# Two more blocks of queries turned by DMA, and gates' weights shared by both halves of a batch

## The chip, the core and the metric

The kernel runs on one core of a Trainium2 chip. The metric is the device time of one execution in microseconds (us). The engines of a core work side by side, each through its own queue in order: TensorE (PE, with its weight loads PEld), VectorE (DVE), ScalarE (ACT), GpSimd (POOL) and SyncE (SP), whose queue here issues nearly all DMAs. They wait for each other through semaphores.

## The reference

A transformer layer over 8 sequences of 1024 rows and 512 features, in float32. First attention with 16 heads of 32 features, causal, on the normalized rows, added to the input; then a gated recurrence on the normalized sum, added again. The recurrence runs over the 8 sequences as its time steps; the 1024 rows are its batch.

```python
def attn(query, in_proj_weight, out_proj_weight):        # query: layernorm(x), 8 x 1024 x 512
    q, k, v = ...                                         # 16 heads of 32
    scores = jnp.einsum('bhqd,bhkd->bhqk', q / math.sqrt(D), k)
    scores = jnp.where(causal[None, None], scores, -jnp.inf)
    attn = jax.nn.softmax(scores, axis=-1)
    return jnp.einsum('bhqk,bhkd->bhqd', attn, v) @ out_proj_weight.T   # heads joined first

def step(c, xt):                                          # xt: one sequence of z', 1024 x 512
    ft = jax.nn.sigmoid(xt @ wf.T + c @ uf.T + bf)
    it = jax.nn.sigmoid(xt @ wi.T + c @ ui.T + bi)
    gt = jnp.tanh(xt @ wc.T + c @ uc.T + bc)
    return ft * c + it * gt, None

x = x + attn(layernorm(x))
z = layernorm(x)                                          # z' below
c_final, _ = lax.scan(step, c0, z)
x = x + jnp.tanh(z @ wo.T + c_final @ uo.T + bo)
```

## The kernel before

**Precision.** Every float32 operand of a product is split into two float16 tiles, high and low part, and a product is three matmuls (high x high, high x low, low x high). `three` issues them for four blocks of 128 features: 12 matmuls of 512 columns, in four planned operations of three.

**Stages.** For each sequence b: normalization and a transpose by DMA into tile zT, one per half of 512 rows (`ln1`); projections to q, k and v in four groups of four heads (`proj`); attention for eight pairs P of heads (64 pairs in all); `out_proj`, whose sum with the input is stored as X1, normalized (z') and turned by DMA into tile z2T; and the gates of the recurrence (`recur`). After the last sequence the output stage runs. Gates of one sequence run beside the attention of the next, so that TensorE always has several kinds of work to choose from.

**Attention in two passes.** The first pass (`a_group`, nine groups per pair, listed in GA) computes scores with queries on the partitions, in the PSUM tile sa (one slot of 1024 columns, two banks), and VectorE reduces them to the maximum of each row. `m_rows` turns the maxima and puts them as two more rows under q. The second pass (`b_group`) computes the scores again with keys on the partitions, in the PSUM tile sb (one slot of 1024 columns), now with the maximum subtracted; ScalarE takes exp (tile e), GpSimd sets the masked half of diagonal blocks to zero, and `split_e` makes the two float16 parts (tile P: ScalarE the high, GpSimd the low). `times_v` multiplies these by v, and `finish` divides by the sum. For the first 16 pairs (MASKED) the mask is added by small matmuls of TensorE instead, in both passes.

**Turned rows.** From pair 20 on (TURNED), queries 896 to 1023 of both heads (query block 7) take another way (`turned_rows`): their scores are computed once, with queries on the partitions, in sb; VectorE masks and reduces, ScalarE takes exp with the row's own maximum as bias, `split_e` splits, and a DMA transposes the 128 x 2048 float16 tile into a second slot of P. Their first-pass groups (0, 7) and (1, 7) fall away, and BANKS lists how the other query blocks are packed into sb.

**Gates.** `recur(t)` goes through its two halves of 512 rows one after the other; in each, through four blocks of features and three gates, 12 units. A unit loads its weights from device memory into tile wf (512 KB, two slots), runs 12 matmuls on z2T and, from t = 1 on, 12 on cs, the split state, and ScalarE and VectorE update the state C.

**Order.** The code records every step as an operation with engine, estimated duration, due time `at`, and the buffers that it reads, writes and holds. `Plan.schedule` then writes out each engine's order: it takes again and again the operation that can start first by its own estimates and, among equals, the one due first. Rings (R) have a fixed number of slots; a buffer takes a slot at its first operation. Due times come from TAU, the length of a pair, and t_a, t_b and t_batch, the times of the first pass, the second pass and a batch. The result is one fixed order per engine, which the chip follows. So moved due times or another number of slots change the order everywhere.

Lines in the profile: L519 is `three`, L566 the products of v, L645 first-pass scores, L647 and L755 mask matmuls, L655 masked maxima and L653 plain ones, L712 scores of turned rows, L717 and L718 their maximum and its scaling, L753 second-pass scores, L758 and L721 exp, L730 and L731 the split, L767 masking on GpSimd, L695 `times_v`, L837 the sum after out_proj, L815 the high part of an attention output, L341 and L343 transposing and plain DMAs.

Of the kernel before, what the change touches and what calls it, by code (L numbers as in the profile page):

```python
# [76 lines left out]
class Plan:  # L77
# [3 lines left out]
    def op(self, eng, dur, fn, r=(), w=(), at=0.0, size=None, hold=(), after=(), alt=None, port=None):  # L81
        o = Op()
        o.alt = alt or {}
        o.port = eng == "POOL" if port is None else port
        o.eng, o.dur, o.fn, o.at, o.size, o.seq = eng, dur, fn, at, size, len(self.ops)
        o.pre, o.succ, o.bufs = {}, [], set(hold)
        for p in after:
            o.pre[p] = 1
        for write, items in ((False, r), (True, w)):
            for x in items:  # L90
                b, key = x if isinstance(x, tuple) else (x, None)
                o.bufs.add(b)
                keep = []
                for k, p, pw in b.acc:
                    hit = key is None or k is None or k == key
                    if hit and (write or pw) and p is not o:
                        o.pre[p] = 1
                    if not (write and hit and (key is None or k == key)) or p is o:
                        keep.append((k, p, pw))
                keep.append((key, o, write))  # L100
                b.acc = keep
        for b in o.bufs:
            b.left += 1
        self.ops.append(o)
        return o

    def schedule(self):
# [19 lines left out]
        while left:  # L127
            best = None
            for e, l in avail.items():
                t = clock[e]  # L130
                pick = None
                for o in l:
# [10 lines left out]
                    ok = True  # L143
                    for b in o.bufs:
                        if b.ring is not None and b.slot is None:
                            q = b.ring
                            if not q.free or (q.fifo and q.queue[0] is not b) or any(x.left for x in q.over):
                                ok = False
                                break
                            f = max([min(q.free)[0]] + [x.end for x in q.over])  # L150
# [47 lines left out]
def layer(ctx, tc, x_in, wqkvT, woT, ffn, woffT, uoffT, vecs, bo, inc, out):  # L198
# [58 lines left out]

    def ring(name, n, shape, dtype, fifo=True, pool_=sb):
        return Ring([pool_.tile(shape, dtype, name=f"{name}{i}") for i in range(n)], fifo)

    def cut(raw, at, n, shape, dtype, fifo=True):
# [12 lines left out]
    raw = {n: sb.tile([128, w * 512], F32, name=n) for n, w in (("zsr", 4), ("natr", 4), ("er", 4), ("Pr", 8), ("stkr", 12), ("wxr", 6))}  # L274
    rz = cut(raw["zsr"], 0, 2, [128, 2, 2, 512], F16, False)
    rn = cut(raw["natr"], 0, 2, [128, 2, T], F16)
    re_ = cut(raw["er"], 0, 2, [128, T], F32)
    rp = cut(raw["Pr"], 0, 4, [128, 2, T], F16, False)
# [8 lines left out]
        "zT": ring("zT", 3, [128, 4, 2, KE, 128], F16),  # L287
# [6 lines left out]
        "e": re_,  # L294
        "P": rp,
        "m": ring("m", 2, [128, 2, 8], F32),
        "m1": ring("m1", 4, [128, 2], F32),
# [12 lines left out]
        "sa": ring("sa", 1, [128, T], F32, True, ps2),  # L310
        "sb": ring("sb", 1, [128, T], F32, True, ps2),
# [11 lines left out]
    R["ty"] = Ring(big("er", 1024) + big("Pr", 1024), over=[re_, rp])  # L323
# [11 lines left out]
    def new(tag):  # L335
        return R[tag].buf()
# [10 lines left out]
    TAU = 33  # L347
    X_SH, X_RAMP, X_G = 40, 12, 6
    T0 = 70
# [152 lines left out]
    def ln1(b, after=()):  # L502

        at0 = -300.0 if b == 0 else t_a(18 * G * b) - 2 * TAU - 60.0 - X_SH * max(0.0, 1 - 4 * b / X_RAMP)
# [75 lines left out]
    def stack_load(P):  # L580
# [9 lines left out]
        if p == 0:  # L590
# [4 lines left out]
    MASKED = 16  # L595
# [13 lines left out]
    AHEAD = 12  # L609
    TURN_KB = 900  # L610
    BANKS = [[(1, 0, 4, 3), (1, 3, 4, 1)], [(1, 1, 4, 3), (1, 3, 5, 1)], [(1, 2, 4, 3), (1, 3, 6, 1)],
             [(1, 4, 4, 3), (1, 6, 6, 1)], [(1, 5, 5, 2), (0, 2, 2, 2)], [(0, 1, 1, 3), (0, 3, 3, 1)], [(0, 0, 0, 4)]]

    def turned(P):
        return P >= TURNED

    def a_group(n):

        P, gi = divmod(n, 9)
        if turned(P) and len(GA[gi]) == 1:  # L620
# [82 lines left out]
    def turned_rows(P, h, at):  # L703
# [3 lines left out]
        pp, e, W, m1 = new("sb"), new("e"), new("P"), new("m1")  # L707

        def fn():
            q, k = t()[:96, 0], t()[:96, 1]  # L710
            for lo in (0, 512):
                pe.matmul(pp()[:, lo : lo + 512], q[:, h, 896:1024], k[:, h, lo : lo + 512], start=True, stop=True)  # L712

        op("PE", 0.435, fn, [(t, j) for j in range(3)], [pp], at)

        def top():
            dve.tensor_tensor_reduce(pp(), pp(), tri, 1.0, NEG, ALU.add, ALU.max, m1()[:, 0:1])  # L717
            dve.tensor_scalar(m1()[:, 1:2], m1()[:, 0:1], TSN, ebias, ALU.mult, ALU.add)  # L718

        op("DVE", 1.55, top, s("TS"), [pp, m1], at)  # L720
        op("ACT", 1.2, lambda: act.activation(e(), pp(), AF.Exp, bias=m1()[:, 1:2], scale=TS), [pp, m1, *s("TS")], [e], at)  # L721
# [4 lines left out]
        items = [(lambda hl, kb=kb: T_()[:, hl, kb * 128 : kb * 128 + 128], kb, 7) for kb in range(8)]  # L726
        return lambda at: times_v(s_, 2 * p + h, 1, items, [T_], at)
# [5 lines left out]
    def b_group(P, banks, at):  # L733
# [5 lines left out]
        for i, group in enumerate(banks):  # L739
            off = i * 512  # L740
            for h, j, kb, q0, nq in group:
                if q0 == kb:
                    diag.append(off)
                parts.append((h, j, kb, q0, off, nq * 128))
# [4 lines left out]
        def fn():  # L749
            q, k = t()[:98, 0], t()[:98, 1]  # L750
            for h, j, kb, qb0, off, w in parts:
# [6 lines left out]
        op("ACT", 1.2, lambda: act.activation(e(), pp(), AF.Exp, bias=ebias, scale=TS), [pp, *s("TS")], [e], at)  # L758
# [14 lines left out]
        for h, j, kb, qb0, off, w in parts:  # L773
            items = [(lambda hl, o=off + x * 128: W()[:, hl, o : o + 128], kb, qb0 + x) for x in range(w // 128)]
            times_v(s_, 2 * p + h, j, items, [(W, 0), (W, 1)], at + 4.0)

    def b_pair(P):
        if not turned(P):
            for i, banks in enumerate(GB_):
                b_group(P, [[(h, j, kb, max(kb, 4 * j), 4 * j + 4 - max(kb, 4 * j)) for h, j, kb in g] for g in banks], t_b(9 * P + i))  # L780
            return
        banks = [[(h, *x) for x in b] for h in range(2) for b in BANKS]
        late = []
        for i in range(9):
            at = t_b(9 * P + i)
            if i % 4 == 0 and i < 8:
                late.append(turned_rows(P, i // 4, at - AHEAD))
            else:
                k = 2 * (i - 1 - i // 5)
                b_group(P, banks[k : k + 2], at)  # L790
                if i in (3, 7):
                    late.pop()(at + 4.0)
# [60 lines left out]

    def recur(t):
        start = t_batch(t + 1) + (140 if t == NB - 2 else 50)
        span = 8 * TAU
        tag = "pj" if t < NB - 1 else "pt"
        for half in range(2):
            begin = ()
            for fq in range(KE):  # L860
                c = C[:, fq, half * 512 : half * 512 + 512]
                key = (state, (fq, half))
                for i, g in enumerate((0, 2, 1)):
                    un = fq * 3 + g
                    w = new("wf")
                    at = start + span * (12 * half + fq * 3 + i) / 24
                    dma(w, lambda un=un: SF()[un], at - 8.0, r=[(SF, (un, 0)), (SF, (un, 1))], w=[w], size=512)
                    if fq == i == 0 and t:
                        cs = csplit(t, half, at - 5.0)
                    zt, p = z2T[t, half], new(tag)  # L870
                    three(p, p, lambda b, k, zt=zt: zt()[:, :, b, k], lambda a, k, w=w: w()[:, 0, a, k], 512, lambda k: [zt, w], at, last=t == 0,
                          after=tanh.get((t - 1, half), ()))
                    if t:
                        three(p, p, lambda b, k, cs=cs: cs()[:, b, k], lambda a, k, w=w: w()[:, 1, a, k], 512,
                              lambda k, cs=cs: [(cs, (k, 0)), (cs, (k, 1)), w], at, first=False)
                    bb = bias if t else bias0
                    o = new("g2") if g == 2 else p
                    tanh[t, half] = (op("ACT", 0.75, lambda o=o, p=p, g=g, bb=bb, fq=fq: act.activation(o(), p(), AF.Tanh, bias=bb[:, g, fq : fq + 1], scale=UG[g]),  # L878
                       [p, *s(("gate", g), ("b0", g, fq))], [o], at),)
                    marks.append(tanh[t, half])  # L880
                    if g == 0:
                        if t:
                            op("DVE", 0.7, lambda p=p, c=c: dve.scalar_tensor_tensor(c, p(), 1.0, c, ALU.add, ALU.mult), [p], [key], at)
                        else:
                            op("DVE", 0.7, lambda p=p, c=c, fq=fq: dve.tensor_scalar(c, p(), 1.0, vec[:, 4, fq : fq + 1], ALU.add, ALU.mult),
                               [p, *s("vec")], [key], at, after=cw_ops)
                    elif g == 2:
                        gg = o
                    else:
                        op("DVE", 0.7, lambda p=p, gg=gg: dve.scalar_tensor_tensor(p(), p(), 1.0, gg(), ALU.add, ALU.mult), [gg], [p], at)  # L890
                        op("DVE", 0.7, lambda p=p, c=c: dve.scalar_tensor_tensor(c, p(), 2.0 ** t, c, ALU.mult, ALU.add), [p], [key], at)
# [139 lines left out]
    for s_ in range(NS):  # L1031
# [3 lines left out]
        if g == G - 1:  # L1035
            out_proj(b)
# [4 lines left out]
    END = t_batch(NB) + 240  # L1041
# [27 lines left out]
    dma(bob, lambda: bo.partition_broadcast(128), END, w=[bob])  # L1069
# [109 lines left out]
```

## Time and profile before

| what | value |
|---|---|
| median of 3 runs | 2691.12 us (2685.93 to 2691.55) |
| the profiled execution | 2684.05 us |
| its span, first to last instruction | 2682.0 us |
| mean granted TensorE clock | 0.991 |
| longest wait of TensorE in all, on VectorE's maxima (sa, L645 after L653) | 18.0 us, 27 times |
| DMA, mean | 179 GB/s |
| transposes of probabilities | 88 |
| loads of gates' weights | 192 of 512 KB |

How to read it: a line of a group gives source line, engine, operation, output <- input with tile names, how often, busy time and mean duration. Busy times of matmuls overlap, since they are pipelined, so the distance between starts says more than a duration. A line in order of time has the start, the time from the first start to the last end of the merged instructions, and their number. A wait is named by what waited and what released it last. One unit of the second pass is a `b_group` or a `turned_rows`; each pair has nine.

### The profile page before, as it was taken

What the parts mean: (1) busy time and instruction counts of PE and PEld (TensorE: products, weight loads), DVE (VectorE), ACT (ScalarE), POOL (GpSimd) and SP (SyncE); (2) the same over time, 40 slices, a digit from 0 to 9 for tenths busy, and PEclk for the clock granted to TensorE, in tenths of its full rate; (3) what the DMA queues carried; (4) which work ended last, traced back from release to release, by engine and by line L of the source; (5) the groups of instructions that cost most, each with busy time, mean ns of one, the idle gap of its engine ahead of it and who ended that gap; (6) DMA issues with size and microseconds to landing.
All of it is one profiled execution on the core that took longest, in us unless ns stands there. A gap on an engine that the chain in (4) does not pass through costs nothing. (4 is left out here: it accounts for less than half of the span.)

```text
span 2682.0 us, 59783 instructions
## 1 busy us (share of the span) xinstructions
PE 2599.8 (97%) x23677; PEld 1484.9 (55%) x23677; DVE 1821.0 (68%) x4373; ACT 1835.0 (68%) x2286; POOL 1563.9 (58%) x1214
## 2 busy tenths in 40 slices
PE   5889999999999999999999999999999999999999
PEld 3555665665555555555555555555555555544444
DVE  4898877787776767676676667676676776432455
ACT  3697879887777777777777677776776777522222
POOL 3475777777766667676767666676666767410000
PEclk9899999999999999999999999999999999999999
DMA  8566576557666876688758876687766765574565
GB/s 241 175 173 190 148 189 186 154 165 195 158 160 170 200 190 167 166 190 205 183 147 189 192 193 160 165 201 199 177 153 160 199 162 126 146 200 151 195 228 212
DMA packets 535304, 479.97 MB, mean 179 GB/s; under 512 B 402160, under 2 KB 402160, under 8 KB 531440
## 3 DMA queue, kind: packets, MB, share of 16 engines
q1 hardware_dynamic: 533936, 474.06, 67.5%
q8 instruction: 185, 3.03, 0.5%
q10 hardware_dynamic: 1088, 2.10, 0.2%
q14 instruction: 95, 0.78, 0.1%
HBM read 270.54 MB, written 108.53 MB: 141 GB/s over the span
## 5 line engine op out<-in xcount | busy, mean ns | idle before, releaser
L731 POOL TENSOR_TENSOR Pr<-er,Pr 128x1024 f16<-128x1024 f32 x565 | 1207.6, 2140 | 481.7 <-ACT Pr L730 404.6
L758 ACT ACTIVATE er<-sb,ebias,usc 128x1024 f32<-128x1024 f32 x488 | 586.6, 1202 | 155.5 <-PE sb L753 123.7
L730 ACT ACTIVATE Pr<-er 128x1024 f16<-128x1024 f32 x576 | 605.2, 1054 | 50.0 <-POOL er L767 36.1
L519 PEld LDWEIGHTS <-wf 128*128 128x128 f16 x4320 | 398.6, 97 | 416.9 <-DMA wf<-SF 6.1
L655 DVE CUSTOM_DVE_ANT_0 sa<-sa,tri 128x768 f32<-128x768 f32 (+7 forms) x680 | 478.5, 704 | 174.2 <-PE sa L645 162.1
L519 PE MATMUL pj<-z2T,wf 128*128 128x512 f16 x2016 | 496.5, 379 | 3.7 <-DVE natr L551 1.1
L519 PE MATMUL pj<-cs,wf 128*128 128x512 f16 x1728 | 421.7, 379 | 0.0
L519 PE MATMUL pj<-zT,wxr 128*128 128x512 f16 x1536 | 383.3, 384 | 5.0 <-DMA zT<-zsr 3.3
L695 PEld LDWEIGHTS <-Pr 128*128 128x128 f16 x9216 | 323.6, 96 | 100.3 <-POOL Pr L731 6.2
L695 PE MATMUL av<-vt,Pr 128*128 128x65 f16 (+1 forms) x9216 | 339.9, 185 | 4.3 <-POOL Pr L731 2.8
L645 PE MATMUL sa<-stkr 96*128 96x512 f16 (+3 forms) x1348 | 299.9, 322 | 19.9 <-DVE m L653 18.0
L753 PE MATMUL sb<-stkr 98*128 98x128 f16 (+3 forms) x1624 | 306.8, 296 | 9.3 <-ACT er L758 8.4
L519 PEld LDWEIGHTS <-wxr 128*128 128x128 f16 x1728 | 160.7, 98 | 180.4 <-issue 14.1
L653 DVE TENSOR_REDUCE m<-sa 128x1 f32<-128x256 f32 (+2 forms) x248 | 177.7, 753 | 54.0 <-PE sa L647 53.0
L767 POOL TENSOR_SCALAR_AFFINE_SELECT er<-er 128x256 f32<-128x256 f32 (+2 forms) x384 | 140.1, 383 | 119.0 <-ACT er L758 117.9
L645 PEld LDWEIGHTS <-stkr 96*128 96x128 f16 x1360 | 123.7, 98 | 128.8 <-issue 23.7
L753 PEld LDWEIGHTS <-stkr 98*128 98x128 f16 x1624 | 141.7, 97 | 96.0 <-issue 9.6
L566 PE MATMUL pj<-wxr,zT 128*128 128x128 f16 x3072 | 191.0, 220 | 2.9 <-ACT wxr L425 1.9
L566 PEld LDWEIGHTS <-zT 128*128 128x128 f16 x3072 | 179.0, 99 | 12.8 <-issue 3.7
L453 POOL TENSOR_TENSOR zsr<-z,zsr 128x512 f16<-128x512 f32 x120 | 141.7, 1181 | 70.8 <-ACT zsr L452 64.1
L519 PE MATMUL pj<-wo,aT 128*128 128x512 f16 x768 | 174.2, 379 | 1.1 <-DVE wxr L837 0.8
L717 DVE CUSTOM_DVE_ANT_0 sb<-sb,tri 128x1024 f32<-128x1024 f32 x88 | 108.6, 1234 | 90.7 <-PE sb L712 87.5
(171 smaller groups left out, 2797.3 us busy)
## 6 DMA issues: line engine op xcount, KB each, us to landing
wf<-SF SPq DMA_DIRECT2D x192, 512.0 KB, 4.0
stkr<-QK SPq DMA_DIRECT2D x192, 256.0 KB, 4.8
QK<-natr SPq DMA_DIRECT2D x64, 512.0 KB, 4.7
wxr<-x SPq DMA_DIRECT2D x112, 256.0 KB, 4.2
wxr<-SQ SPq DMA_DIRECT2D x93, 256.0 KB, 3.1
VD<-vs SPq DMA_DIRECT2D x64, 264.0 KB, 2.9
vt<-VD SPq DMA_DIRECT2D x32, 528.0 KB, 5.2
stkr<-X SPq DMA_DIRECT2D x16, 1024.0 KB, 7.3
```

The costliest lines, as they stand in the source:

```text
L453: o = op("DVE", 0.85, lambda: eng[o.eng].tensor_tensor(zs()[:, i, 1], z(), zs()[:, i, 0], ALU.subtract), [z, (zs, (i, 0))], [(zs, (i, 1))] ...
L519: pe.matmul(pv(), sv(a, k), mv_(b, k), start=first and k == 0 and i == 0, stop=last and k == KE - 1 and i == 2)
L566: pe.matmul(p()[:, n * 128 : n * 128 + 128], zt()[:, n, a, k], w[2]()[:, c, k], start=i == 0, stop=i == 3 * KE - 1)
L645: pe.matmul(pp()[:, lo:hi], q[:, h, qb * 128 : qb * 128 + 128], k[:, h, lo - off : hi - off], start=True, stop=not last, skip_group_check= ...
L653: dve.tensor_reduce(m()[:, h, qb : qb + 1], pp()[:, off : off + w], AX.X, ALU.max)
L655: dve.tensor_tensor_reduce(pp()[:, off : off + w], pp()[:, off : off + w], tri[:, T - w :], 1.0, NEG, ALU.add, ALU.max, m()[:, h, qb : qb ...
L695: pe.matmul(av()[:, o + 32 * hl : o + 65], stat(hl), v()[:, kb, i, 32 * hl : 65], start=c == 1, stop=c == total, skip_group_check=True)
L730: op("ACT", 1.06, lambda: act.activation(W()[:, 0], e(), AF.Copy), [e], [(W, 0)], at)
L731: lo = op("POOL", 2.18, lambda: eng[lo.eng].tensor_tensor(W()[:, 1], e(), W()[:, 0], ALU.subtract), [e, (W, 0)], [(W, 1)], at, alt={"DVE": ...
L753: pe.matmul(pp()[:, off : off + w], k[:, h, kb * 128 : kb * 128 + 128], q[:, h, qb0 * 128 : qb0 * 128 + w], start=True, stop=not last, ski ...
L758: op("ACT", 1.2, lambda: act.activation(e(), pp(), AF.Exp, bias=ebias, scale=TS), [pp, *s("TS")], [e], at)
L767: pool.affine_select(out=x, in_=x, pattern=[[0, n], [1, 128]], compare_op=ALU.is_ge, fill=0.0, base=0, channel_multiplier=-1)
```

## The change

- `turned` now lists pairs (head, query block). From pair 20 on, head 0 also has query blocks 6 and 0 (queries 768 to 895 and 0 to 127) turned, from pair 60 on head 1 too. Blocks 6 and 0 are one call of `turned_rows`: 896 and 128 columns side by side in one tile, in sa instead of sb. Their first-pass groups (0, 6)+(0, 0), and (1, 6)+(1, 0), fall away. BANKS has a second packing for a head with three blocks turned, five banks instead of seven. Transposes come 20 units of due time ahead instead of 12, the products 4 behind the due time of the row.
- Tile P has six slots instead of four; zT has two instead of three. e and P lie in one raw buffer.
- In `recur`, except for the last sequence, the units of the two halves alternate, and a unit of half 1 uses the weights that half 0 loaded.
- The mask matmuls end at pair 14 instead of 16.
- Due times: TAU 32.75 instead of 33, T0 76 instead of 70, other ramps at the front, gates due 60 (200 for the last but one) after their batch instead of 50 (140), the end 260 instead of 240 behind. The calls of the second pass and of out_proj are sorted by due time before they are recorded. The planner counts slots when one operation takes several, and keeps buffers in the order of use.

```diff
-    rp = cut(raw["Pr"], 0, 4, [128, 2, T], F16, False)
+    rp = cut(big_, 0, 8 if MERGE else 6, [128, 2, T], F16, False)
+    re_ = cut(big_, 6144, 2, [128, 2, T], F16)
...
-        "zT": ring("zT", 3, [128, 4, 2, KE, 128], F16),
+        "zT": ring("zT", 2, [128, 4, 2, KE, 128], F16),
...
-    TAU = 33
-    X_SH, X_RAMP, X_G = 40, 12, 6
-    T0 = 70
+    TAU = 32.75
+    X_SH, X_RAMP, X_G = 40, 8, 7
+    T0 = 76
...
-    MASKED = 16
+    MASKED = 14
...
-    AHEAD = 12
+    TURNED2 = 20
+    TURNED3 = 60
+    PROMPT = 4
+    AHEAD = 20
...
+        2: [[(0, 1, 4)], [(1, 1, 4)], [(2, 2, 4)], [(3, 3, 3), (5, 5, 1)], [(4, 4, 2), (0, 5, 1), (1, 5, 1)]],
...
     def turned(P):
-        return P >= TURNED
+        if P < TURNED:
+            return []
+        return [(h, q) for h in range(2) for q in ((7, 6, 0) if (P >= TURNED2 and (h == 0 or P >= TURNED3)) else (7,))]
...
-        if turned(P) and len(GA[gi]) == 1:
+        if any(x in turned(P) for x in GA[gi]):
...
-    def turned_rows(P, h, at):
+    def turned_rows(P, h, qbs, at):
...
-        pp, e, W, m1 = new("sb"), new("e"), new("P"), new("m1")
+        pp, e, W, m1 = new(TURN_PS if len(qbs) > 1 else "sb"), new("e"), new("P"), new("m1")
+        parts, off = [], 0
+        for qb in qbs:
+            parts.append((qb, off, qb * 128 + 128))
+            off += qb * 128 + 128
...
+        def exps():
+            for i, (qb, off, w) in enumerate(parts):
+                act.activation(e()[:, off : off + w], pp()[:, off : off + w], AF.Exp, bias=m1()[:, 2 + i : 3 + i], scale=TS)
...
+            for x, qbs in enumerate(((7,), (6, 0))[: two[h]]):
+                if PROMPT < 0:
+                    turn(h, qbs, a0 + x * step - AHEAD, end - 0.5 * step + 4.0 + 0.1 * x)
+                else:
+                    turn(h, qbs, a0 + x * step - AHEAD, a0 + x * step + PROMPT)
...
+    SHARE = 1
+
     def recur(t):
-        start = t_batch(t + 1) + (140 if t == NB - 2 else 50)
+        start = t_batch(t + 1) + (200 if t == NB - 2 else 60)
...
+        if t < NB - 1 and SHARE:
+            units = [(half, fq, i, (2 * (3 * fq + i) + half) / 24) for fq in range(KE) for i in range(3) for half in range(2)]
+        else:
+            units = [(half, fq, i, (12 * half + 3 * fq + i) / 24) for half in range(2) for fq in range(KE) for i in range(3)]
+        wfs, css, ggs = {}, {}, {}
+        for half, fq, i, x in units:
...
+            if un in wfs:
+                w = wfs.pop(un)
+            else:
+                w = new("wf")
+                if t < NB - 1 and SHARE:
+                    wfs[un] = w
+                dma(w, lambda un=un: SF()[un], at - 8.0, r=[(SF, (un, 0)), (SF, (un, 1))], w=[w], size=512)
...
-            out_proj(b)
+            events.append((t_batch(b + 1) + 6.0, len(events), out_proj, (b,)))
+    for _, _, fn, a in sorted(events, key=lambda x: x[:2]):
+        fn(*a)
...
-    END = t_batch(NB) + 240
+    END = t_batch(NB) + 260
```

## The prediction

> **What bounds the kernel.** I read the totals first, then the same engines by stretches of the span, then what TensorE waits for, then its instructions in order of time.
>
> ```profile
> PE 2599.8 (97%) x23677; PEld 1484.9 (55%) x23677; DVE 1821.0 (68%) x4373; ACT 1835.0 (68%) x2286; POOL 1563.9 (58%) x1214
> ```
>
> By stretches (columns: stretch, its length, then busy us of TensorE, weight loads, VectorE, ScalarE, GpSimd, the granted clock, the DMA share, GB/s):
>
> ```profile
> 603.00:2144.00 1541.00, 1536.53 (x14441) 885.94 (x14440) 1083.22 (x2832) 1140.92 (x1407) 1037.44 (x863) 1.00 0.73 179
> 0.00:67.00 67.00, 39.79 (x313) 24.12 (x314) 33.15 (x69) 25.38 (x36) 20.67 (x25) 0.97 0.82 241
> 67.00:402.00 335.00, 302.40 (x3433) 195.68 (x3432) 281.34 (x610) 265.97 (x336) 219.63 (x128) 0.93 0.63 175
> 402.00:603.00 201.00, 195.66 (x2157) 121.15 (x2155) 152.74 (x336) 179.70 (x219) 147.83 (x85) 1.00 0.62 169
> ```
>
> From 603 to 2144 us TensorE is idle for 4.5 of 1541 us; ScalarE, the next, is at 74%. The idle time is at the front: 27.2 us before 67, 32.6 us up to 402, where the clock is 0.93 too. A busy row could hide slow, overlapping matmuls, so the distance from start to start is what counts:
>
> ```profile
> 1003.01 2.85 PE L566 MATMUL pj<-wxr,zT 128*128 128x128 f16 x48
> 1005.70 0.60 PE L645 MATMUL sa<-stkr 96*128 96x512 f16 x3
> 1006.13 0.60 PE L753 MATMUL sb<-stkr 98*128 98x384 f16 x4
> 1006.57 2.76 PE L519 MATMUL pj<-z2T,wf 128*128 128x512 f16 x12
> 1009.16 0.60 PE L645 MATMUL sa<-stkr 96*128 96x512 f16 x3
> ```
>
> No gap stands between different tasks. 1024 columns of scores take 0.43 to 0.44 us whether they are three matmuls (1005.70 to 1006.13) or four (1006.13 to 1006.57); twelve of 512 columns take 2.59 us, 216 ns each; 48 of 128 columns take 2.69 us, 56 ns each. So TensorE streams without a pause, and in this stretch the time is the sum of its matmuls. What shortens that sum shortens the span, unless it opens a gap.
>
> **Part 1, queries 6 and 0 turned too.** Head 0 of pairs 20 to 63 and head 1 of pairs 60 to 63: 44 + 4 = 48 times, the first-pass group (6, 0) in tile sa (1024 columns) falls away. Its 1024 columns are now computed once, in turned_rows, and the second pass loses the same two sets of blocks: in the orders of instructions, sa's score matmuls stay as many, sb's lose 48 x 1024 columns. Saved: 48 x 0.435 = 20.9 us of TensorE. The new BANKS also cut 240 matmuls out of sb (longer ones take their place); three or four for 1024 columns cost the same above, so nothing for that.
>
> [...]
>
> What stands against it, off TensorE: the reductions by VectorE move with the rows, plus 48 of L718 (0.273 us) = 13 us; ScalarE's one exp of 1.2 us becomes two (896 wide, about 1.05 by width, and 128 wide, 0.27 as L815's 128-wide copy), 48 x 0.12 = 6 us; GpSimd loses 96 diagonal blocks and wins 32 (Part 3). Of 1541 us these engines use 1083, 1141 and 1037, so all of it is covered: nothing. If that cover were gone, ScalarE's 6 us would count in full.
>
> New waits. A turned row holds sa (its only slot) through 1.10 + 0.30 + 2 x 0.14 + 0.27 us on VectorE and 1.3 on ScalarE, about 3.3 us; queued behind it on TensorE is the next first-pass group, and behind that everything, since the queue is in order. By the changed order, costed with the rows above, the work between is 3.1 us at the least, 3.7 at the lowest tenth, 4.75 in the median. So a few rows stall for tenths: 0 to 48 x 0.5 = 24 us at worst, and I take 1, near 0, because turned rows in sb held it 2.85 us with 2.97 us between at the least, and no sb wait is listed between 603 and 2144 us.
>
> The transposes: 48 more on SP, each 2.9 us of the queue (median of the 88), against 84 loads of wf fewer (0.34 us each). Landing takes these times (median) from the issue:
>
> ```profile
> wf<-SF SPq DMA_DIRECT2D x192, 512.0 KB, 4.0
> Pr<-Pr SPq DMA_TRANSPOSE x88, 5.0
> zT<-zsr SPq DMA_TRANSPOSE x36, 4.9
> z2T<-zsr SPq DMA_TRANSPOSE x28, 5.4
> ```
>
> The longest of the 88 took 9.6 us. By the orders, the TensorE work from issue to first use was at least 7.4 us and is now at least 14.0 (AHEAD 12 to 20), and six P slots instead of four hold the rows meanwhile. Cost: nothing; if landings passed 14 us, TensorE would wait for the excess. The queue's bytes go down (25 MB more in transposes, 44 MB less in wf).
>
> **Part 2, gates' weights shared by both halves.** Matmuls and weight loads on TensorE stay (4320 with wf); only DMA is saved, which nobody waited for (1.0 us in all before 2345). But half 0 and half 1 of the state now advance together, so both z2T slots stay held until a batch's gates end, and out_proj of half 1 comes late. Before, the order left 116 to 132 us of TensorE work between the last product of half 1 and the first gate that reads it (batches 1 to 6); now 16.2 (batches 2 to 5), in batch 0 only 9.6, batch 1 15.5. What this has to cover is seen at one boundary:
>
> ```profile
> 1528.64 2.75 PE L519 MATMUL pj<-wo,aT 128*128 128x512 f16 x12
> 1531.43 0.75 DVE L837 SCALAR_TENSOR_TENSOR wxr<-pj,usc,wxr 128x512 f32<-128x512 f32 x1 [1.12 <-PE pj L519]
> 1537.87 2.33 SPq L341 DMA_TRANSPOSE z2T<-zsr  x1
> ```
>
> The products end at 1531.2, the transpose is issued at 1537.9 and lands 5.4 later: 12.1 us. So 16.2 suffices, and batch 0 stalls 12.1 - 9.6 = 2.5. Half 0 keeps 16 or more there. The last batch: its half 0 leaned on 15.6 us and now has 10.4, because the gates of batch 6 are done before; the same chain there took from 2345.6 (fourth of eight products that begin at 2335.22, 2.59 each) to 2352.5 + 4.9, so 11.8, and stalls 1.4. Together 4 us; the bounds are 0 and the case of rival A.
>
> **Part 3, pairs 14 and 15 masked off TensorE.** 64 mask matmuls fall away at 0.056: 3.6 us; VectorE and GpSimd take the masks (32 blocks of 0.29 us), at 76% and 74% between 402 and 603. Nothing for that; if ScalarE, at 89% there, sets that stretch instead, the 3.6 us are lost.
>
> **Part 4, due times and rings** (TAU, T0, ramps, recur's starts, two zT slots). They only reorder. By the orders, 15.7 us of filler on TensorE (eight products of proj, eight of v, eight of out_proj) move from before to behind the 81st unit of the second pass, that is, out of the stretch that has gaps. If VectorE and ScalarE set the pace there, TensorE idles up to 15.7 us longer; if not, nothing, and better packing could win some of the 32.6 idle. TensorE at 90%, ahead of VectorE at 84%, is the nearest row: I take 0, with -10 to +15.7 for the range. zT's two slots leave 7.8 us or more from the last transpose to its use in batches 2 to 7, where 8 to 9 was enough before: nothing.
>
> **Sum.** -20.9 - 3.6 + 1 + 4 = -19.5 us. The profiled execution took 2684.05 (span 2682.0), so 2664.5; the runs' median lies 1.0026 above it, 2691.12, which makes 2671.6, say 2671.
>
> **Rivals.** A: the shared weights turn the batch boundaries into stalls. For: z' of half 1 lost its cover; in another place, the last transpose of half 1 was issued at 657.19 after an out_proj product at 639.9, 17.3 us, with 5.4 to land 22.7, unhurried. Against: there nobody waited, while the changed order has it urgent. If it took 22.7 everywhere, the seven boundaries cost 13.1 + 7.2 + 4 x 6.5 + 2 (batch 6 has 20.7) = 48, and the time is 2691 - 24.5 + 48 = 2715. It decides from about 25 us, 3.5 per boundary, a chain of some 19 us. B: the front loses the filler, +15.7: 2687, no change. For: TensorE's longest wait there is on VectorE (sa after m, 15 us up to 402). Against: the moved filler brought VectorE and ScalarE work of its own. C: the front packs better and nothing stalls: 2691 - 24.5 - 10 = 2657.
>
> **Chances.** Forecast 0.73, C 0.08, A 0.10, B 0.09. A measurement of this kernel tells about 0.2% (5.4 us) from no change; so faster is forecast and C, 0.81, the same B, slower A. The range: from below C by the fastest run's distance (2685.93 against 2691.12), 2652, up to 2690 for B with some stalls of A; it leaves out A and the outer ends of C and of the forecast.
>
> **What would show it.** TensorE's busy time near 2575 with 64 and 240 fewer matmuls; idle from 603 to 2144 still below 10 us; no TensorE wait on the transposes of probabilities. Wrong if waits of L519's gates on z2T or zT add up to over 20 us, if idle before 402 passes 75, or if sa's release after turned rows becomes TensorE's longest wait.

## The result and the profile after

| what | before | changed |
|---|---|---|
| median, 8 runs each, side by side | 2687.94 us (2684.44 to 2692.99) | 2702.42 us (2693.70 to 2706.66) |
| ratio to before, 95% interval | | 1.0050 (1.0037 to 1.0063) |
| span of the profiled execution | 2682.0 us | 2701.1 us (that execution took 2702.79) |
| mean granted TensorE clock | 0.991 | 0.986 |

The change made the kernel about 14 us slower; 2671 was forecast, and 2702 lies outside the range of 2652 to 2690. The totals of the changed kernel:

```profile
PE 2589.6 (96%) x23373; PEld 1463.7 (54%) x23373; DVE 1858.0 (69%) x4452; ACT 1843.0 (68%) x2334; POOL 1562.2 (58%) x1227
```

The 304 matmuls are gone (23677 to 23373), yet TensorE's busy time fell by 10 us only, and VectorE's rose by 37. The work itself costs what it did before, as TensorE's instructions in order of time show:

```profile
1006.19 0.23 PE L695 MATMUL sa<-ident,mh 128*32 128x128 f16 x1
1006.35 2.12 PE L535 MATMUL pj<-z2T,wf 128*128 128x512 f16 x9
1008.30 0.81 PE L535 MATMUL pj<-cs,wf 128*128 128x512 f16 x3
```

Nine matmuls of 512 columns from start to next start take 1.95 us, 217 ns each. So the rates hold, and the time must have gone into gaps. By stretches (stretch, length, busy us of TensorE, weight loads, VectorE, ScalarE, GpSimd, granted clock, DMA share, GB/s):

```profile
67.00:402.00 335.00, 300.63 (x3379) 194.72 (x3377) 274.68 (x588) 260.28 (x326) 216.76 (x120) 0.90 0.60 164
402.00:603.00 201.00, 190.50 (x2044) 115.12 (x2042) 156.92 (x364) 173.95 (x214) 145.39 (x94) 1.00 0.54 144
603.00:2144.00 1541.00, 1518.49 (x14232) 866.77 (x14231) 1104.75 (x2857) 1148.33 (x1448) 1035.20 (x867) 1.00 0.73 171
```

From 603 to 2144 us TensorE is now idle for 22.5 us (4.5 before), and from 402 to 603 for 10.5 (5.3 before). What it waited for between 603 and 2144 us, longest first (what waited, what released it: us in all, times, longest), first in the kernel before, the three longest:

```profile
PE pj L519 <- DVE natr L551: 1.1, 1, 1.1
PE av L695 <- POOL Pr L731: 1.1, 3, 0.4
PE sa L669 <- DVE mh L667: 0.8, 2, 0.4
```

then in the changed one, the four longest:

```profile
PE pj L535 <- DVE natr L567: 4.9, 4, 1.2
PE sa L695 <- DVE mh L693: 4.0, 5, 0.8
PE sa L671 <- ACT big__99 L760: 3.2, 9, 0.6
PE sa L695 <- ACT big__99 L760: 3.0, 4, 0.8
```

In the changed kernel L535 is `three`, L567 the low part of q and k, L671 the first-pass scores, L681 their masked maxima, L693 and L695 the maxima and their transpose in `m_rows`, L745 scores of turned rows, L753 and L754 their maximum and its scaling, L760 their exp, L776 and L777 the split, L799 and L805 second-pass scores and exp, L976 the state. All four are for tile sa or for VectorE's queue; none is on z2T. One line that can stand behind them shows in the groups, forms kept apart (times run | busy us, mean ns | idle before):

```profile
L754 DVE TENSOR_SCALAR m<-m,usc,ebias 128x2 f32<-128x2 f32 x48 | 46.6, 971 | 1.7
L754 DVE TENSOR_SCALAR m<-m,usc,ebias 128x1 f32<-128x1 f32 x88 | 24.0, 273 | 3.2
```

In the kernel before, this line knew one form only:

```profile
L718 DVE TENSOR_SCALAR m<-m,usc,ebias 128x1 f32<-128x1 f32 x88 | 24.0, 273 | 3.2
```

The scaling of the two maxima of a double row (queries 6 and 0) is one instruction on 128x2 numbers. It takes 0.971 us on average, where the same instruction on 128x1 takes 0.273. One of them in order of time, VectorE first:

```profile
1053.97 0.14 DVE L753 DVE_READ_ACCUMULATOR2_ANT m<- 128x1 f32 x1
1054.14 1.86 DVE L754 TENSOR_SCALAR m<-m,usc,ebias 128x2 f32<-128x2 f32 x1
1055.92 0.28 DVE L888 TENSOR_TENSOR os<-av,os 128x128 f16<-128x128 f32 x1
1056.12 0.16 DVE L693 SCALAR_TENSOR_TENSOR mh<-m,mh 128x16 f16<-128x16 f32 x1
```

GpSimd at that time:

```profile
1053.86 2.12 POOL L777 TENSOR_TENSOR big__99<-big__99 128x1024 f16<-128x1024 f32 x1
```

ScalarE:

```profile
1056.10 1.45 ACT L760 ACTIVATE big__99<-sa,m,usc 128x896 f32<-128x896 f32 x2 [2.33 <-DVE m L754]
```

TensorE:

```profile
1057.60 0.22 PE L695 MATMUL sa<-ident,mh 128*32 128x128 f16 x1 [0.75 <-ACT big__99 L760]
```

GpSimd's split began at 1053.86 and ended at 1055.98; the scaling began 0.28 us later and ended at 1056.00. Of the 48, 22 took 0.29 us; none of these lies wholly within one GpSimd instruction. The other 26 took 0.39 to 2.07 us, and all of them end 0.02 to 0.03 us after the end of a GpSimd instruction that was running when they began. So the two-column form waits here for the end of GpSimd's running instruction. ScalarE, idle for 2.33 us, starts right behind it, sa is released late, and TensorE stands 0.75 us. With the order fixed, this returns from batch to batch: the same 0.75 us at 1057.60, 1357.70, 1657.81 and 1957.90.

What in the chip makes this form wait, and not the one-column form (0.27 to 0.28 us, 88 times of 88 in this trace), is shown by no row.

DMA went as forecast (KB each, or none, then median us to landing):

```profile
wf<-SF SPq DMA_DIRECT2D x108, 512.0 KB, 3.8
big__99<-big__99 SPq DMA_TRANSPOSE x136, 4.6
```

**Lost time by batch.** Where gaps arise is seen best so: take the time of a batch's first sum after out_proj, and subtract the TensorE work that the order has put ahead of it, at the prediction's rates (0.216 us per 512 columns, 0.435 per 1024 columns of scores, 0.056 per 128 columns) and 0.054 for the two matmuls of a block with v, whose starts lie 25 to 30 ns apart. The last rate is a little low, but it is the same in every row, so the differences between rows hold. All are worked out, in us, from one execution each; "per batch" is the mean from batch 2 to 6.

| kernel | work | lost by batch 0 | by 1 | by 2 | per batch | by the end |
|---|---|---|---|---|---|---|
| before | 2544.1 | 90.8 | 102.9 | 106.8 | 3.6 | 137.9 |
| changed | 2519.6 | 99.8 | 117.4 | 125.8 | 8.0 | 181.5 |
| extra rows off | 2540.4 | 99.2 | 116.9 | 126.5 | 3.2 | 155.9 |
| scaling by column | 2519.6 | 100.3 | 118.5 | 126.1 | 4.9 | 168.9 |
| due times alone | 2544.1 | 101.9 | 120.8 | 127.7 | 7.7 | 187.1 |
| new settings | 2523.9 | 98.4 | 118.2 | 123.2 | 2.4 | 154.0 |

Work fell by 24.5 us, losses rose by 43.6; together the 19.1 us of the spans. 19 of the losses arise by batch 2, the rest by 4.4 per batch and at the end.

### The profile page after: what moved, and what is told of

It reads as the page before. It is cut to its first block, busy times and chain, and to the rows that moved or that the text cites. A ratio compares the mean times of both kernels' runs of the same rounds, so it can differ in the third digit from the quotient of the medians.

```text
span 2701.1 us, 59247 instructions
## 1 busy us (share of the span) xinstructions
PE 2589.6 (96%) x23373; PEld 1463.7 (54%) x23373; DVE 1858.0 (69%) x4452; ACT 1843.0 (68%) x2334; POOL 1562.2 (58%) x1227
## 4 chain that ended last, share of the span: by engine, by line
PE 69%; DVE 7%; ACT 2%; issue 2%; DMA 1%; POOL 0%; SPq 0%; POOLq 0%; DVEq 0%; ACTq 0%
PE pj L535 37%; PE pt L535 7%; PE av L721 6%; PE sb L799 5%; PE sa L671 4%; PE pj L582 4%; PE av L535 4%; PE sb L745 1%; DVE sa L753 1%; DVE m L754 1%; DVE sb L753 1%; DVE mh L693 1%; DVE sa L681 1%; ACT big__99 L760 1%; ACT big__99 L805 1%
## 5 line engine op out<-in xcount | busy, mean ns | idle before, releaser
L777 POOL TENSOR_TENSOR big__99<-big__99 128x1024 f16<-128x1024 f32 x567 | 1210.1, 2139 | 519.7 <-ACT big__99 L776 478.8
L776 ACT ACTIVATE big__99<-big__99 128x1024 f16<-128x1024 f32 x576 | 603.9, 1053 | 55.1 <-POOL big__99 L814 34.6
L535 PEld LDWEIGHTS <-wf 128*128 128x128 f16 x4320 | 399.9, 97 | 443.0 <-issue 15.0
L805 ACT ACTIVATE big__99<-sb,ebias,usc 128x1024 f32<-128x1024 f32 x440 | 528.3, 1201 | 134.3 <-PE sb L799 101.5
L681 DVE CUSTOM_DVE_ANT_0 sa<-sa,tri 128x640 f32<-128x640 f32 (+7 forms) x616 | 436.3, 708 | 196.6 <-PE sa L671 176.6
L535 PE MATMUL pj<-z2T,wf 128*128 128x512 f16 x2016 | 496.1, 379 | 5.4 <-DVE C L967 3.3
L535 PE MATMUL pj<-cs,wf 128*128 128x512 f16 x1728 | 419.8, 379 | 0.0
L535 PE MATMUL pj<-zT,wxr 128*128 128x512 f16 x1536 | 381.1, 383 | 13.6 <-DVE natr L567 7.1
L721 PEld LDWEIGHTS <-big__99 128*128 128x128 f16 x9216 | 322.8, 97 | 92.9 <-issue 8.4
L721 PE MATMUL av<-vt,big__99 128*128 128x65 f16 (+1 forms) x9216 | 338.1, 185 | 3.8 <-DVE os L888 2.3
L671 PE MATMUL sa<-stkr 96*128 96x512 f16 (+3 forms) x1204 | 272.6, 325 | 24.8 <-DVE m L679 18.0
L799 PE MATMUL sb<-stkr 98*128 98x128 f16 (+3 forms) x1384 | 280.3, 307 | 14.9 <-ACT big__99 L805 8.1
L535 PEld LDWEIGHTS <-wxr 128*128 128x128 f16 x1728 | 161.9, 98 | 186.6 <-issue 24.1
L814 POOL TENSOR_SCALAR_AFFINE_SELECT big__99<-big__99 128x256 f32<-128x256 f32 (+2 forms) x396 | 138.3, 367 | 144.5 <-ACT big__99 L805 138.0
L679 DVE TENSOR_REDUCE m<-sa 128x1 f32<-128x256 f32 (+2 forms) x216 | 154.8, 753 | 50.7 <-PE sa L673 50.3
L535 PE MATMUL pj<-wo,aT 128*128 128x512 f16 x768 | 174.2, 379 | 2.9 <-DVE vs L588 1.0
L799 PEld LDWEIGHTS <-stkr 98*128 98x128 f16 x1384 | 123.0, 98 | 96.1 <-issue 18.9
L671 PEld LDWEIGHTS <-stkr 96*128 96x128 f16 x1216 | 109.5, 98 | 116.9 <-issue 27.9
L753 DVE CUSTOM_DVE_ANT_0 sb<-sb,tri 128x1024 f32<-128x1024 f32 x88 | 109.1, 1239 | 43.5 <-PE sb L745 38.5
```

Source lines behind the costliest of these rows:

```text
L535: pe.matmul(pv(), sv(a, k), mv_(b, k), start=first and k == 0 and i == 0, stop=last and k == KE - 1 and i == 2)
L671: pe.matmul(pp()[:, lo:hi], q[:, h, qb * 128 : qb * 128 + 128], k[:, h, lo - off : hi - off], start=True, stop=not last, skip_group_check= ...
L679: dve.tensor_reduce(m()[:, h, qb : qb + 1], pp()[:, off : off + w], AX.X, ALU.max)
L681: dve.tensor_tensor_reduce(pp()[:, off : off + w], pp()[:, off : off + w], tri[:, T - w :], 1.0, NEG, ALU.add, ALU.max, m()[:, h, qb : qb ...
L721: pe.matmul(av()[:, o + 32 * hl : o + 65], stat(hl), v()[:, kb, i, 32 * hl : 65], start=c == 1, stop=c == total, skip_group_check=True)
L753: dve.tensor_tensor_reduce(pp()[:, off : off + w], pp()[:, off : off + w], tri[:, T - w :], 1.0, NEG, ALU.add, ALU.max, m1()[:, i : i + 1])
```

## Experiments

**Extra rows off.** All parts of the change but queries 6 and 0:

```diff
-    TURNED2 = 20
-    TURNED3 = 60
+    TURNED2 = 64
+    TURNED3 = 64
```

> The changed kernel with queries 6 and 0 back on the two-pass way (only query block 7 turned); rings, due times, shared gates' weights and masks as changed. TensorE gets 48 x 0.435 = 20.9 us of work back. If Part 1 is innocent and paid in full, the idle time between 603 and 2144 us stays near 22 us and the time is 2702 + 21 = 2723. If the extra rows bring the new waits (sa held until ScalarE's exp, maxima transposed late), idle there falls to 4 to 8 us and the time is 2702 + 21 - 16 = about 2707. If the new waits come from the written order as a whole, idle falls by some part and the time lies between, 2705 to 2720.

Measured: 2694.17 us, ratio to before 1.0022 (1.0012 to 1.0032). The stretches:

```profile
67.00:402.00 335.00, 301.01 (x3379) 195.05 (x3377) 275.09 (x589) 260.89 (x326) 217.19 (x120) 0.90 0.60 164
603.00:2144.00 1541.00, 1533.92 (x14435) 884.56 (x14434) 1052.15 (x2822) 1138.63 (x1409) 1048.81 (x871) 1.00 0.66 158
```

That is below all three of the times expected. With 20.8 us more work on TensorE it is 8 us faster than the changed kernel, so the order with the rows loses some 29 us more than the one without: TensorE's idle time in the long stretch is 7.1 instead of 22.5. But it is still slower than before, and its losses up to batch 2 are those of the changed kernel. This points at two causes: one that comes with the rows, one elsewhere and early.

**Weights apart.** The changed kernel, each half loading its own:

```diff
-    SHARE = 1
+    SHARE = 0
```

> The changed kernel with each half of a batch loading its own gates' weights again, halves one after the other; all else as changed. TensorE's work is the same. If the shared weights make the loss (rival A of the prediction), the waits at the batch boundaries go and the time falls by 15 to 25 us, to about 2682. If they are innocent and the order as a whole decides, another order comes out of the same settings: other small waits, no fall, and more likely a rise of some 10 to 60 us, as the due times were not made for it.

Measured: 2751.07, 1.0231 (1.0217 to 1.0245). The long stretch, and its longest TensorE wait:

```profile
603.00:2144.00 1541.00, 1497.08 (x13898) 853.39 (x13897) 1063.67 (x2778) 1131.32 (x1412) 1025.10 (x855) 0.99 0.78 187
```

```profile
PE pj L535 <- DVE C L976: 12.2, 17, 2.6
```

TensorE idles 43.9 us there, and without sharing 49 us are lost. Of its waits on loads of weights (wf) the profile lists 0.5 us ahead of the output stage, so the 49 are not TensorE waiting for the extra loads; they come with another order, in which the halves no longer alternate. That the due times were set for alternating halves may be part of it; that was not taken apart. Rival A falls, all the more as no wait on z2T shows in the changed kernel.

**Double rows in sb.** The changed kernel, with the scores of queries 6 and 0 in the other tile:

```diff
-    TURN_PS = "sa"
+    TURN_PS = "sb"
```

> The changed kernel with the rows of queries 6 and 0 in the PSUM tile sb like those of 7, instead of sa. TensorE's work is the same. If sa held by these rows is the cause, first-pass scores and the transposed maxima no longer wait for their exp (6.2 us listed between 603 and 2144, and 4.0 of late maxima), and the time falls by about 10 us to 2692. If the order as a whole decides, those waits are replaced by others at sb, and the time does not fall: 2700 to 2740.

Measured: 2730.76, 1.0158 (1.0143 to 1.0174). The scaling is as before in two columns:

```profile
L754 DVE TENSOR_SCALAR m<-m,usc,ebias 128x2 f32<-128x2 f32 x48 | 42.8, 892 | 1.7
```

37 of the 48 take more than 0.30 us, and all 37 end 0.02 to 0.03 us after a GpSimd instruction. TensorE is idle for 35.0 us in the long stretch instead of 22.5. In sb the kernel is 28 us worse, so the other tile is no remedy. But the wait of the scaling is still there and the order is a new one, so this run does not tell what holding sa costs by itself.

**Less work in the order of before.** Kernel before, its order kept:

```diff
-                for i, (a, b) in enumerate(((0, 0), (0, 1), (1, 0))):
+                for i, (a, b) in enumerate(((0, 0), (0, 1), (1, 0))[:terms]):
...
-                          after=tanh.get((t - 1, half), ()))
+                          after=tanh.get((t - 1, half), ()), terms=2 if 1 <= t <= 5 and (fq + i) % 4 == 0 else 3)
```

> The kernel before, its order of operations untouched; it leaves out the low-times-high products of z' and the gates' input weights in 30 of the gate units of batches 1 to 5, that is 120 matmuls of 512 columns, 120 x 0.216 = 25.9 us of TensorE, spread over the same stretch as the 48 groups of the change. If TensorE's sum sets the time as the prediction's first step said, and what failed is the new order, the time falls by 22 to 26 us, to about 0.991 of the kernel before. If another engine or the DMA is close behind TensorE, it falls by less than 10 us.

Measured: 2667.22, 0.9922 (0.9908 to 0.9935). The long stretch, with 7.5 us idle:

```profile
603.00:2144.00 1541.00, 1533.48 (x14576) 888.67 (x14575) 1100.35 (x2871) 1155.80 (x1427) 1053.18 (x878) 1.00 0.73 182
```

The 120 matmuls are 25.9 us at 216 ns, and 21 came out (17 to 25 by the interval), a little less than the 22 expected at the least. So the prediction's first step stands: in this order, work taken off TensorE shortened the time by most of its sum.

**Scaling by column.** The changed kernel, its order untouched, the one instruction on two columns written as two on one:

```diff
-            dve.tensor_scalar(m1()[:, 2 : 2 + n], m1()[:, 0:n], TSN, ebias, ALU.mult, ALU.add)
+            for i in range(n):
+                dve.tensor_scalar(m1()[:, 2 + i : 3 + i], m1()[:, i : i + 1], TSN, ebias, ALU.mult, ALU.add)
```

> The changed kernel, its order untouched; only the scaling of the two maxima of a turned row (L754, one VectorE instruction on 128 x 2) is written as two instructions on 128 x 1. In the changed kernel's profile 22 of the 48 instructions on 128 x 2 took 0.29 us and the others up to 2.07, ending when GpSimd's running instruction ends; the 88 on 128 x 1 all took 0.27 to 0.28. If this wait for GpSimd is what makes the extra rows cost more than they save, all now take 0.27, VectorE loses some 20 us of busy time, the waits of first-pass scores and maxima on the rows' exp (6.2 us listed) and on late maxima (4.0) go, idle between 603 and 2144 falls from 22.5 to about 10, and the time falls by 10 to 16 us, to about 2689. If the rows wait anyway because sa is held through two reductions and two exps, the time stays within 4 us of 2702.

Measured: 2687.16 (12 runs), 0.9995 (0.9984 to 1.0007). The scaling in the groups:

```profile
L755 DVE TENSOR_SCALAR m<-m,usc,ebias 128x1 f32<-128x1 f32 x184 | 45.7, 270 | 3.2
```

The long stretch, and TensorE's waits in it:

```profile
603.00:2144.00 1541.00, 1527.42 (x14334) 873.27 (x14333) 1097.83 (x2929) 1160.33 (x1460) 1044.81 (x879) 1.00 0.74 173
```

```profile
PE sa L695 <- DVE mh L693: 4.0, 5, 0.8
PE pj L535 <- DVE natr L567: 3.1, 5, 0.6
```

None of the 184 takes over 0.275 us. VectorE executes 48 instructions more and is busy 24 us less; the waits for sa on exp of the turned rows (6.2 us) are gone, and that on natr fell from 4.9 to 3.1; 15 us of time are back, and with them the whole loss against before. The idle time fell to 13.6 us, not to the expected 10: the 4.0 us on late maxima (mh) stayed, so the wait of the scaling is not what makes them. What stays was not taken apart.

**Rings back, extra rows off.** As the first experiment, with three slots of zT and four of P:

```diff
-        "zT": ring("zT", 2, [128, 4, 2, KE, 128], F16),
+        "zT": ring("zT", 3, [128, 4, 2, KE, 128], F16),
...
-    rp = cut(big_, 0, 8 if MERGE else 6, [128, 2, T], F16, False)
+    rp = cut(big_, 0, 4, [128, 2, T], F16, False)
```

> The kernel of the run with the extra rows off, with three zT slots and four P slots as before; due times, shared weights and masks as changed. To be compared with that run (2694): if the third zT slot is what the front misses, the time lost by the first out_proj falls by some 9 us and the total to about 2685. If due times and order decide, the loss only moves to another place and the time stays at 2694 or rises by up to 10.

Measured: 2703.88, 1.0052 (1.0032 to 1.0073), 10 us slower than with two and six. By batch 2 it has lost 121.7 us instead of 126.5, so the two rings, changed together, explain at most 5 us of the early loss, and more is lost later (161.8 by the end instead of 155.9).

**Due times alone.** Kernel before, with the changed kernel's due times and nothing else:

```diff
-    TAU = 33
-    X_SH, X_RAMP, X_G = 40, 12, 6
-    T0 = 70
+    TAU = 32.75
+    X_SH, X_RAMP, X_G = 40, 8, 7
+    T0 = 76
...
-        start = t_batch(t + 1) + (140 if t == NB - 2 else 50)
+        start = t_batch(t + 1) + (200 if t == NB - 2 else 60)
...
-    END = t_batch(NB) + 240
+    END = t_batch(NB) + 260
```

(The lead of the normalization, 60 to 44, and the start of out_proj, 3 to 6, go with them.)

> The kernel before with the new due times alone (TAU, T0, ramps, starts of gates, out_proj and the end). TensorE's work is exactly that of before. If due times only reorder at no cost, as the prediction took them (0, bounds -10 and +15.7), the time stays within 0.4% of before. If the written order is delicate, so that due times made for one set of operations do not fit another, it rises by 1 to 2%, 27 to 54 us, spread over the front, the batch boundaries and the end of attention.

Measured: 2730.08, 1.0154 (1.0133 to 1.0174). The long stretch and its longest TensorE wait:

```profile
603.00:2144.00 1541.00, 1519.38 (x14259) 875.91 (x14258) 1039.67 (x2764) 1121.75 (x1382) 1027.03 (x852) 1.00 0.71 177
```

```profile
PE pj L519 <- DVE C L891: 9.8, 11, 1.1
```

The same work in another order costs 42 us, and by batch 2 the loss is 127.7, as in the changed kernel (125.8). So the due times alone bring an early loss of that size, with nothing else changed. The changed kernel with the due times of before was not run, so that they are the cause there too is likely but not shown.

**TAU nudged.** Kernel before, one number:

```diff
-    TAU = 33
+    TAU = 33.1
```

> The kernel before with TAU 33.1 instead of 33, nothing else. The work is the same. If the written order is delicate, this alone costs 0.3 to 0.7% (8 to 19 us), in small waits of TensorE at the end of attention and in each batch, as large as the change under study. If not, nothing that can be measured changes.

Measured: 2700.98, 1.0041 (1.0023 to 1.0059). A due time moved by 0.3% costs 13 us. Losses by batch 2 are 110.6, then 5.2 per batch instead of 3.6.

**Mended, with new settings.** Scaling by column, and the rows begin at pair 22, head 1 has none extra, and transposes come 14 units ahead:

```diff
-    TURNED = 20
+    TURNED = 22
...
-    TURNED3 = 60
+    TURNED3 = 64
...
-    AHEAD = 20
+    AHEAD = 14
```

> The changed kernel with the scaling of maxima column by column, and with three settings: transposes 14 units of due time ahead instead of 20, turned rows from pair 22 instead of 20, head 1's extra rows never. TensorE's work is 4.3 us more than with the mended scaling alone. If due times and order decide what is left, the waits per batch shrink from 4.9 us of lost time to the 3.5 of before, and the time falls to about 2679, 0.3% below the kernel before. If the extra rows themselves bring waits that no setting takes away, it stays at 2687 or above.

Measured: 2677.85 (12 runs), 0.9967 (0.9957 to 0.9977), faster than both kernels. Its long stretch, and the longest TensorE wait in it:

```profile
603.00:2144.00 1541.00, 1538.38 (x14467) 881.78 (x14466) 1106.81 (x2948) 1161.23 (x1469) 1044.50 (x879) 1.00 0.73 172
```

```profile
PE sa L671 <- DVE m L681: 1.8, 3, 0.8
```

With 42 double rows in sa TensorE is idle for 2.6 us in 1541, less than before the change. So the double rows, the weights shared and the six slots of P do fit. Per batch 2.4 us are lost; 16 us more than before are lost by batch 2, and as much by the end, so the early loss is all that is left of the damage. Which of the three settings did it was not tried.

**Two columns in before.** Kernel before, its order untouched; the maximum of each turned row is copied into a second column and the scaling done on both, so that only its width and a 0.15 us copy are new:

```diff
-            dve.tensor_scalar(m1()[:, 1:2], m1()[:, 0:1], TSN, ebias, ALU.mult, ALU.add)
+            dve.tensor_copy(m1()[:, 1:2], m1()[:, 0:1])
+            dve.tensor_scalar(m1()[:, 2:4], m1()[:, 0:2], TSN, ebias, ALU.mult, ALU.add)
```

> The kernel before, order untouched; the scaling of a turned row's maximum runs on 128 x 2 instead of 128 x 1 (the second column is a copy, one more small VectorE instruction, and is not used). If VectorE's instruction on two columns waits for GpSimd's running one, about half of the 88 now take up to 2.1 us, their mean is near 1 us, and TensorE idles more between 603 and 2144 us (4.5 before): the time rises by 0.2 to 0.6%, 5 to 16 us. If the length in the changed kernel came from something else of its rows (tile sa, two reductions), all 88 take 0.3 us and the time stays within 0.1%.

Measured: 2743.04, 1.0207 (1.0185 to 1.0229). The two lines in the groups, and the long stretch:

```profile
L719 DVE TENSOR_SCALAR m<-m,usc,ebias 128x2 f32<-128x2 f32 x88 | 106.4, 1210 | 3.2
L718 DVE COPY m<-m 128x1 f32<-128x1 f32 x88 | 13.5, 154 | 3.0
```

```profile
603.00:2144.00 1541.00, 1499.55 (x14005) 859.81 (x14005) 1128.53 (x2814) 1105.03 (x1360) 1007.45 (x841) 1.00 0.70 172
```

67 of the 88 took more than 0.30 us, up to 2.17, and all 67 end 0.02 to 0.03 us after a GpSimd instruction's end. The sign was expected, the size was not: 56 us instead of 5 to 16. VectorE got 96 us of extra time (106.4 + 13.5 - 24.0), so 58% of it came out as time; in the changed kernel the mending took 24 us off VectorE, of which 15 came out, 62%. So VectorE's idle third covered less than half of it.

## Why the prediction was wrong

**What bounds the kernel: right.** 304 matmuls and 24.5 us of work are gone, at the rates that were read, and the experiment with less work shows that such a sum comes out to four fifths. It says nothing of gaps, and the prediction's own condition, "unless it opens a gap", decided.

**Part 1, mis-sized.** "Plus 48 of L718 (0.273 us) = 13 us ... nothing". The row was that of the one-column form; the change makes it two columns. It measured 46.6 us, and the cover did not hold: the excess lies between the scores in sa and the exp that releases it, with everything behind that in TensorE's queue, and ahead of natr in VectorE's. Where the sum had +1 for rows that hold sa, the scaling alone costs 15 us, shown by mending it and, from the other side, by putting it into the kernel before. That VectorE's share was 70% was no reason to call an instruction covered that stands on the way to sa. Nor had the trace of before a 128x2 scaling, and its cost was not bounded from both sides.

The other steps of Part 1 held but one small price: the two exps take 1.45 us together instead of 1.32, since the 128-wide one takes 0.45 us and not the 0.27 of L815's copy. Landing of the transposes has a median of 4.6 us, and no TensorE wait on them is among the longest. The 3.3 us of sa are no trouble in themselves, as the version with new settings shows.

**Part 4, wrong.** "They only reorder ... I take 0, with -10 to +15.7". Alone they cost the kernel before 42 us, and TAU by itself, moved by 0.1, 13. The step that failed is the bound: it counted filler that moves out of the front, while a new due time reorders every batch. In the changed kernel 19 us more than before are lost by batch 2, some 9 of them already by batch 0, and the same with the extra rows off or the scaling mended. That is rival B's place and more than its price of 15.7; its mechanism is not shown. (B's reading of the front was not quite right either: the longest wait before 402 us is one of 17.8 us at the very start, in both kernels alike, and only then come the 15 us for sa.) At the front TensorE waits up to 603 us, as before, 18.0 us for VectorE's maxima, and the wait on the DMA of the maxima's rows grew from 0.5 to 4.6 us (the wait at the very start is left out):

```profile
PE sa L671 <- DVE m L679: 18.0, 21, 2.4
PE sb L799 <- ACT big__99 L805: 7.7, 16, 1.3
PE sb L799 <- DMA stkr<-mt: 4.6, 4, 1.9
```

**Part 2, right that nothing much happens at the boundaries.** 4 us of stalls on turned z' were counted; none on z2T is seen, and 0.5 us on zT, which holds the last batch's. That nobody waits for the loads held too, ahead of the output stage. What was not seen is that the order with halves apart, under these due times, is 49 us slower.

**Part 3** was not tried alone. The stretch from 402 to 603, where it lies, has 5 us more idle time where a gain of 3.6 us was forecast, but the due times moved there too.

**The marks set beforehand.** Busy time near 2575: 2589.6. Idle from 603 to 2144 below 10: 22.5, and this is the mark that gave the error away. Idle before 402 under 75: 62.1, held, though 9 us more were lost there by batch 0. The mark misses them because the granted clock from 67 to 402 was 0.90 (0.93 before): TensorE is busy for nearly as long (300.6 us, 302.4 before) with 54 matmuls fewer. In the version with the scaling mended the same stretch has 0.93, 6 us less busy time, 6 us more idle time and the same loss (100.3), so the lower clock is not the cause. No wait on z2T, 0.5 us on zT and none on the transposes of probabilities among the longest: held. The release of sa after turned rows was to show the error if it became TensorE's longest wait: over the whole execution it did not (18.0 us are on maxima), but from 603 to 2144 us its two rows make 6.2 us together, the most there.

**The account of spans.** Forecast -19.5, measured +19.1, 38.6 apart: 12.6 are the scaling (2701.1 to 2688.5), 19 the loss by batch 2 with the due times, 12 the rest of batches 3 to 7 and the end, less the 5 us of stalls that were counted. The 12 are not taken apart; the due times alone lose 7.7 per batch, so they can be of the same kind, which is not shown. The 19 are put down to the due times by place and size. Which of the due times it is stays open, and with it what a better set would bring.

## What to carry over

Price a changed instruction by the row of its new shape, and where no such row exists, ask whether it can come to wait for a busy neighbour, as VectorE's scaling did here for GpSimd, up to 2.07 us at a time; a third of idle time hid less than half (58 to 62% came out as time) of a delay that stood between a single buffer and an in-order queue. A fixed order is part of the kernel's tuning: due times that "only reorder" can cost more than the work that a change saves, so measure them alone, and compare changes under an unchanged order where that can be had.

## What the runs showed of the hardware

In the changed kernel a `tensor_scalar` on 128x2 float32 numbers, with source and target in on-chip memory, took 0.29 us in 22 cases of 48, in which GpSimd was idle or its running instruction ended within that time; the other 26 ended 0.02 to 0.03 us after GpSimd's running instruction, with up to 2.07 us in all (2.17 with two columns in the kernel before). On 128x1 it took 0.27 to 0.28 us in the same kernel, 88 times of 88, though during 58 of these one GpSimd instruction was running from start to end, and 0.26 to 0.28 with the scaling by column, 184 times of 184. Two narrow instructions were therefore cheaper here than one of twice the width: 0.54 us against 0.97 on average.
